# A spiking recurrence and its product with the table: the first piece of the last step taken from v itself, and v's two tiles exchanged

## The chip, the core and the metric

The kernel runs on one core of a Trainium2 chip. The metric is the time of one execution on the device in microseconds (us). Inputs and outputs lie in the chip's main memory (HBM). TensorE is the matmul engine, VectorE (DVE in the profile) and ScalarE (ACT) work element by element, GpSimd (POOL) issues the gathers, SyncE (SP) issues most transfers, and 16 DMA engines move the data. The matmul's results lie in PSUM, a memory of eight banks of 2 KB in each of 128 partitions; everything else lies in SBUF.

## The reference

`seq` (1024 x 50 indices), `lengths` (1024) and a table of 100001 x 128 numbers come in, with `gamma` and `beta` (128 each). Row 0 of the table counts as zero.

```python
e = emb[seq]                                   # 1024 x 50 x 128
uF = cumsum(e, axis=1) / minimum(t_idx, lengths)
y = (uF - mean) * rsqrt(var + 1e-5) * gamma + beta   # mean and var over the 1024 rows
def step(v, x):                                # 50 steps
    v = v + (x - v) / 2.0
    spike = (v - 1.0 >= 0)
    v = v - spike * 1.0
    return (v, spike)
scores = mean(spikes over the steps) @ emb.T   # 1024 x 100001
```

The output has 409.6 MB. It is written once; the table has 51 MB.

## The kernel before

**Recurrence (lines 172 to 443).** Everything is kept transposed: 128 features in the partitions, the 1024 rows of the batch along the free dimension. In each of the 50 steps `gather` (L204) issues eight indirect DMAs on GpSimd, two steps ahead. TensorE transposes the eight pieces of 128 rows onto a running sum in the PSUM tiles `pre0` and `pre1` (L327), so that the prefix sum is accumulated there; `correct` (L279) subtracts what row 0 of the table put in. VectorE scales each half to `uF` (L338) and takes its statistics (L339, L345). ScalarE and VectorE make 1/sqrt of the variance in a few instructions on 128x1 (L349, L362 to L375), and `a`, which holds it times -2 times a quarter of gamma; the minus sign is met by `uF` being replaced by mean minus uF (L356). Then come the new v = 0.5 x + 0.5 v: `x` (L379, ScalarE) writes 0.5 x into the tile of the new v, `step` (L382, VectorE) adds -0.5 times `negv`, which is minus the v of the step before after its reset.

The reset is made in two instructions. `over` (L293, ScalarE) writes d = v - 1 as bf16; `rest` (L297, VectorE) makes negv = (d >= 0) - v. `spiked` (L300, VectorE) counts (v >= 1) into `count`.

v lies in PSUM, in two tiles of 1024 that take turns, "v0" in even steps and "v1" in odd ones (L385). "v1" was used once before by `zps` (read by ScalarE, L226), "v0" by `rps` (read by VectorE, L245). In steps 42 and 44 the tile "v1" that the step before has left also serves to transpose the first two parts of the table (L397 to L409), and behind the loop it serves as `po1`.

**The last step (t = 49)** is cut in pieces A (128 rows), B (512) and C (384), so that the product with piece A can start early. `rest` of piece A (L320, run in L297) and `near` = -0.5 negv + 0.5 beta (L322) come at its beginning, ahead of uF on VectorE's queue. Then `centred` = (uF - mean) times -0.25 gamma (L352), q (L366, L367), which is -2 / sqrt(var + eps) up to a second-order correction, `vA` = centred q + near (L369) and `countA` (L370, run in L300). q times `centred` is thus half of x without beta. `keep_busy` (L307) puts transposes into an unused tile `warm` between the last transposes of the loop and behind them: the latter, 16 of them, read `near` (L414).

Behind the loop come the first four products, of `countA` with two parts of the table (L424), in `po0` and `po1`, each half with its own eviction (ScalarE L430, the last one VectorE L428) and store. Among them piece B is made in `pre1` (L433 to L436, ending with `countB`), and at the end piece C in a PSUM tile `vC` of the tag "v0" (L440 to L443, ending with `countC`): ScalarE writes it, VectorE adds and counts.

**Product (lines 448 to 533).** The 98 parts of the table (1024 rows of it each) are taken in blocks of 2, 3 or 6. Each part is transposed and split in two numbers of fewer bits (`prepare`, L148), `hi` and `lo` (or `pairs`). For each of the eight groups of 128 batch rows, `product` (L157, matmul in L160) fills a PSUM tile `po` of 1024 with four matmuls, VectorE (L511) and ScalarE (L513) evict in turn into `o` in SBUF, and SyncE stores (L169). The first block starts with group 1, as group 0 was done before: `po_1_0` and `po_1_1` (group 1, parts 0 and 1), then `po_2_0`, `po_2_1` and so on. Groups 1 to 4 multiply by pieces of `countB`, groups 5 to 7 by pieces of `countC`.

**Places in PSUM.** The pools of the recurrence fill all eight banks: `pre0` and `pre1` have banks 0 and 1, `po0` (and `warm`) 2 and 3, "v1" 4 and 5, "v0" 6 and 7. The pool of the product opens when they close, with four tiles of two banks over the same eight. It waits tile by tile: an instruction that writes a new tile waits for the last readers of what lay in its banks. Its first tiles have these places:

| tile | first bank | what lay there | last read by |
|---|---|---|---|
| po_1_0 | 0 | pre0, pre1 | countB (L300) |
| po_1_1 | 6 | vC | countC (L300) |
| po_2_0 | 4 | po1 | L430, L428 |
| po_2_1 | 2 | po0 | L430 |

The schedule is written by hand: each engine runs its instructions in the order of the code. Waits are put in from the tiles that instructions read and write; for PSUM there is a wait also between two engines that only read the same banks. So d of step 48 (L393, run in L293) waits for the count that L392 put ahead of it.

Of the kernel before, what the change touches and what calls it, by code (L numbers as in the profile page):

```python
# [12 lines left out]
F32 = mybir.dt.float32  # L13
# [5 lines left out]
ALU = mybir.AluOpType  # L19

P = 128
BN_EPS = 1e-5
V_TH = 1.0
HALF = 1024
KQ = HALF // P
BANK = 512
# [13 lines left out]
def rec_kernel(  # L40
# [9 lines left out]
    nc = tc.nc  # L50
    B, T = seq.shape
# [17 lines left out]
    countA = const.tile([P, P], F32R, tag="countA", name="countA")  # L69
# [60 lines left out]
    def turned(q, pt):  # L130
        r = rows.pop(q)
        if q == 0:
            nc.vector.memset(r[0:1, :D], 0.0)
        pw = deep(q)
        for k0 in range(0, HALF, P):
            nc.tensor.transpose(pt[:, k0 : k0 + pw], r[:pw, k0 : k0 + D], ident[:pw, :pw])  # L136

    def views(q, pt, hi, lo):
        pw = deep(q)
        return (  # L140
            pt.rearrange("d (k p) -> d p k", k=KQ)[:, :pw, :],
            hi[:, : pw * KQ].rearrange("d (p k) -> d p k", k=KQ),
            lo[:, : pw * KQ].rearrange("d (p k) -> d p k", k=KQ),
        )
# [3 lines left out]
    def prepare(q, pt):  # L148
        turned(q, pt)
        split[q] = hi, lo = free.pop(0)  # L150
        vp, vh, vl = views(q, pt, hi, lo)
        nc.scalar.copy(vh, vp)  # L152
        nc.vector.tensor_tensor(vl, vp, vh.bitcast(F32), ALU.subtract)  # L153
# [18 lines left out]
    with ExitStack() as ph:  # L172
        once = ph.enter_context(tc.tile_pool(name="once", bufs=1))
# [5 lines left out]
        vp = ph.enter_context(tc.tile_pool(name="v", bufs=1, space=bass.MemoryType.PSUM))  # L179
# [5 lines left out]
        r0 = once.tile([P, D], F32, tag="r0", name="r0")  # L185
        nc.sync.dma_start(out=r0, in_=table[0:1, :].to_broadcast([P, D]))
        gb = once.tile([P, 2], F32, tag="gb", name="gb")
# [39 lines left out]
        r0hi = once.tile([P, D], F32R, tag="r0hi", name="r0hi")  # L227
# [18 lines left out]

        hgb = once.tile([P, 3], F32, tag="hgb", name="hgb")
        nc.vector.tensor_scalar_mul(hgb[:, 0:1], gb[:, 0:1], 0.25)
        nc.vector.tensor_scalar_mul(hgb[:, 2:3], gb[:, 0:1], -0.25)
        nc.vector.tensor_scalar_mul(hgb[:, 1:2], gb[:, 1:2], 0.5)  # L250
        eps = once.tile([P, 1], F32, tag="eps", name="eps")
        nc.vector.memset(eps, BN_EPS)
        less = once.tile([P, 1], F32, tag="less", name="less")
        nc.vector.memset(less, -V_TH)
        count = once.tile([P, B], BF16, tag="count", name="count")
        nc.vector.memset(count, 0.0)

        negv = once.tile([P, B], F32, tag="negv", name="negv")
# [31 lines left out]
        def over(t, v):  # L290

            d = lp.tile([P, B], BF16, tag="d", name=f"d_{t}")
            nc.scalar.activation(d, v, AF.Identity, bias=less)  # L293
            return d

        def rest(d, v, cs):
            nc.vector.scalar_tensor_tensor(negv[:, cs], d[:, cs], 0.0, v[:, cs], ALU.is_ge, ALU.subtract)  # L297

        def spiked(out, cs, v):
            nc.vector.scalar_tensor_tensor(out, v, V_TH, count[:, cs], ALU.is_ge, ALU.add)  # L300
# [3 lines left out]
        pieceA, pieceB, pieceC = slice(0, P), slice(P, P + BANK), slice(P + BANK, B)  # L304
# [6 lines left out]
        v = None  # L311
# [4 lines left out]
        for t in range(T):  # L316
            last = t == T - 1
            e = es.pop(t)
            if last:
                rest(d, v, pieceA)  # L320
                near = once.tile([P, P], F32, tag="r0", name="near")
                nc.vector.tensor_scalar(near, negv[:, :P], -0.5, hgb[:, 1:2], ALU.mult, ALU.add)  # L322
            uF = up.tile([P, B], F32, tag="uF", name=f"uF_{t}")
            bs = sp.tile([P, B // BANK, 6], F32, tag="bs", name=f"bs_{t}")
            for h, cs in enumerate(halves):
                for k in range(0, BANK, P):
                    nc.tensor.matmul(  # L327
                        pre[h][:, k : k + P],
                        lhsT=e[:, h * BANK + k : h * BANK + k + P],
                        rhs=ident,  # L330
                        start=False,
                        stop=last,
                        is_transpose=True,
                        skip_group_check=True,
                    )
                    if last and h and k + P < BANK:
                        keep_busy(ident, KQ // 2)
                nc.vector.scalar_tensor_tensor(uF[:, cs], rlen[:, cs], 1.0 / (t + 1), pre[h], ALU.max, ALU.mult)  # L338
                nc.vector.bn_stats(bs[:, h, :], uF[:, cs])  # L339
            if t + 2 < T:  # L340
                gather(t + 2)
            if not last:
                correct(t + 1, l)
            mv = sp.tile([P, 2], F32, tag="mv", name=f"mv_{t}")
            nc.vector.bn_aggr(mv, bs.rearrange("p h s -> p (h s)"))  # L345


            r = sp.tile([P, 1], F32, tag="r", name=f"r_{t}")
            nc.scalar.activation(r, mv[:, 1:2], AF.Sqrt, bias=eps)  # L349
            if last:  # L350
                centred = once.tile([P, P], F32, tag="r0hi", name="centred")
                nc.vector.tensor_scalar(centred, uF[:, :P], mv[:, 0:1], hgb[:, 2:3], ALU.subtract, ALU.mult)  # L352
                w = sp.tile([P, 1], F32, tag="w", name="w")
                nc.vector.tensor_scalar_add(w, mv[:, 1:2], BN_EPS)
            else:
                nc.scalar.activation(uF, uF, AF.Identity, bias=mv[:, 0:1], scale=-1.0)  # L356


            if t and not last:
                rest(d, v, whole)  # L360

            nc.vector.reciprocal(r, r)  # L362
            q = sp.tile([P, 1], F32, tag="q", name=f"q_{t}")
            a = sp.tile([P, 1], F32, tag="a", name=f"a_{t}")
            if last:
                nc.vector.tensor_scalar(q, w, r, r, ALU.mult, ALU.mult)  # L366
                nc.vector.scalar_tensor_tensor(q, q, 3.0, r, ALU.subtract, ALU.mult)  # L367
                vA = once.tile([P, P], F32, tag="r0n", name="vA")
                nc.vector.scalar_tensor_tensor(vA, centred, q, near, ALU.mult, ALU.add)  # L369
                spiked(countA, slice(0, P), vA)  # L370
                nc.vector.tensor_mul(a, q, hgb[:, 0:1])
            else:
                nc.vector.scalar_tensor_tensor(q, mv[:, 1:2], BN_EPS, r, ALU.add, ALU.mult)
                nc.vector.tensor_scalar(q, q, r, 3.0, ALU.mult, ALU.subtract)
                nc.vector.tensor_scalar(a, q, r, hgb[:, 0:1], ALU.mult, ALU.mult)  # L375


            def x(vt, cs):
                nc.scalar.activation(vt, uF[:, cs], AF.Identity, bias=hgb[:, 1:2], scale=a)  # L379

            def step(vt, cs):
                nc.vector.scalar_tensor_tensor(vt, negv[:, cs], -0.5, vt, ALU.mult, ALU.add)  # L382

            if not last:
                vt = vp.tile([P, B], F32, tag=f"v{t % 2}", name=f"v_{t}")  # L385
                x(vt, whole)
                if t:
                    spiked(count, whole, v)
                step(vt, whole)
                v = vt  # L390
                if t == T - 2:
                    spiked(count, whole, v)  # L392
                d = over(t, v)  # L393
                if t + 2 < T:
                    l = only(t + 2)

                if t in (T - 8, T - 6):  # L397
                    q = (t - T + 8) // 2
                    pair(q)
                    prepare(q, vp.tile([P, HALF], F32, tag="v1", name=f"pt_{q}"))  # L400
                    if q == TWICE - 1:
                        for k in range(TWICE):
                            rows[GROUP + ASIDE + k] = first[:, k, :]
                        nc.sync.dma_start(
                            out=first[:, :TWICE, :],
                            in_=table[(GROUP + ASIDE) * HALF : (GROUP + SHIFT) * HALF, :].rearrange(
                                "(q p k) d -> p q (k d)", p=P, k=KQ
                            ),
                        )  # L409
# [6 lines left out]
            nc.scalar.activation(uF[:, cs], uF[:, cs], AF.Identity, bias=mv[:, 0:1], scale=-1.0)  # L416

        po0 = accp.tile([P, HALF], F32, tag="po0", name="po_0_0")
        po1 = vp.tile([P, HALF], F32, tag="v1", name="po_0_1")
        o0 = gp.tile([P, HALF], F32, tag="e", name="o_0_0")  # L420
        o1 = gp.tile([P, HALF], F32, tag="e", name="o_0_1")
        firsts = [(q, po, o, h, cs) for q, po, o in ((0, po0, o0), (1, po1, o1)) for h, cs in enumerate(halves)]
# [14 lines left out]
        rest(d, v, pieceC)  # L437
        for f in firsts:
            first_store(*f)
        vC = vp.tile([P, B - BANK - P], F32, tag="v0", name="vC")  # L440
        x(vC, pieceC)
        step(vC, pieceC)
        spiked(countC, pieceC, vC)  # L443
# [19 lines left out]
    for c, W in enumerate(WIDTHS):  # L463
# [34 lines left out]
        for n in range(NB):  # L498
            if c == 0 and n == 0:
                continue  # L500
            pool, tag, most = turns[blocks % len(turns)]
# [51 lines left out]
```

## Time and profile before

| | us |
|---|---|
| runs shown: lowest, median, highest | 1637.56, 1643.39, 1649.35 |
| the profiled execution's own time | 1576.4 |
| its span, from the first to the last instruction | 1574.6 |
| busy in the span: TensorE | 1128.4 |
| VectorE | 949.3 |
| ScalarE | 673.4 |
| GpSimd | 380.9 |

How to read the lines that follow. In a timeline a line has the start and the time in us from the span's start, the engine, the line of the kernel, the operation, its output and inputs by the program's names, shapes, the count, and in brackets how long the engine stood idle before it and what released it. In the chain that ended last a line has the start, the time, and the engine and line; "issue" is time in which the engine waited for nothing that the profile shows. A helper's instruction has the helper's line: all of `rest` is L297, all of `spiked` L300. Ends of matmuls are modelled; their starts are of more use.

### The profile page before, as it was taken

What the parts mean: (1) busy time and instruction counts of PE and PEld (TensorE: products, weight loads), DVE (VectorE), ACT (ScalarE), POOL (GpSimd) and SP (SyncE); (2) the same over time, 40 slices, a digit from 0 to 9 for tenths busy, and PEclk for the clock granted to TensorE, in tenths of its full rate; (3) what the DMA queues carried; (4) which work ended last, traced back from release to release, by engine and by line L of the source; (5) the groups of instructions that cost most, each with busy time, mean ns of one, the idle gap of its engine ahead of it and who ended that gap; (6) DMA issues with size and microseconds to landing.
All of it is one profiled execution on the core that took longest, in us unless ns stands there. A gap on an engine that the chain in (4) does not pass through costs nothing.

```text
span 1574.6 us, 12255 instructions
## 1 busy us (share of the span) xinstructions
PE 1128.4 (72%) x4464; PEld 799.5 (51%) x4464; DVE 949.3 (60%) x1127; ACT 673.4 (43%) x697; POOL 380.9 (24%) x406
## 2 busy tenths in 40 slices
PE   4544444444445998899888878888878878888884
PEld 2211111111122766677766666666666666666663
DVE  5777777777777655666555555555555545555552
ACT  2333333333333545555444444444444444444442
POOL 7777777777776000000000000000000000000000
PEclk9999999999975999999999999898999999999998
DMA  9711111111121899999999999999999999999998
GB/s 347 264 52 54 52 54 52 53 53 54 52 79 47 337 414 414 423 413 402 428 427 429 427 426 421 421 409 429 421 428 424 402 428 429 414 423 417 426 405 354
DMA packets 51313, 488.12 MB, mean 310 GB/s; under 512 B 10079, under 2 KB 10336, under 8 KB 30004
## 3 DMA queue, kind: packets, MB, share of 16 engines
q1 hardware_dynamic: 30752, 430.86, 65.1%
q0 software_dynamic: 12800, 26.24, 5.7%
q10 hardware_dynamic: 7700, 30.23, 4.7%
q8 instruction: 35, 0.57, 0.1%
q14 instruction: 26, 0.21, 0.0%
HBM read 77.69 MB, written 409.60 MB: 309 GB/s over the span
## 4 chain that ended last, share of the span: by engine, by line
DMA 48%; POOL 18%; PE 15%; issue 8%; DVE 5%; ACT 4%; ACTq 0%; SPq 0%; POOLq 0%; DVEq 0%
DMA scores<-o 42%; POOL e L207 18%; PE po L160 14%; DMA e<-in_L_rec_emb_table,idx 6%; DVE o L511 3%; ACT o L513 3%; DVE pairs L153 1%; ACT pairs L152 0%; PE pt L136 0%; ACT hi L152 0%; DVE lo L153 0%; PE pre L327 0%; DMA idx<-in_r_seq 0%; DVE bs L339 0%; DVE uF L338 0%
## 5 line engine op out<-in xcount | busy, mean ns | idle before, releaser
L511 DVE TENSOR_SCALAR o<-po 128x1024 f32<-128x1024 f32 (+1 forms) x391 | 467.3, 1214 | 329.5 <-DMA scores<-o 187.4
L513 ACT ACTIVATE o<-po 128x1024 f32<-128x1024 f32 x391 | 392.0, 1025 | 506.0 <-DMA scores<-o 362.7
L207 POOL DMA_INDIRECT e<-in_L_rec_emb_table,idx x400 | 380.2, 951 | 123.9 <-issue 112.5
L327 PE MATMUL pre<-ident,e 128*128 128x128 f32 x400 | 179.9, 463 | 227.3 <-DMA e<-in_L_rec_emb_table,idx 227.0
L160 PE MATMUL po<-pairs,countB 128*128 128x512 f32 (+1 forms) x1120 | 292.8, 408 | 57.8 <-ACT o L513 57.8
L160 PE MATMUL po<-pairs,countC 128*128 128x512 f32 (+1 forms) x840 | 240.1, 433 | 59.4 <-ACT o L513 53.4
L160 PEld LDWEIGHTS po<-pairs,countB 128*128 128x128 f32 x1120 | 211.8, 194 | 119.2 <-ACT o L513 76.7
L327 PEld LDWEIGHTS pre<-ident,e 128*128 128x128 f32 x400 | 73.4, 184 | 337.1 <-DMA e<-in_L_rec_emb_table,idx 336.4
L160 PEld LDWEIGHTS po<-pairs,countC 128*128 128x128 f32 x840 | 168.1, 208 | 112.1 <-ACT o L513 65.5
L153 DVE TENSOR_TENSOR pairs<-pt,pairs 128x1024 fp32r<-128x1024 f32 x70 | 85.2, 1218 | 94.9 <-ACT pairs L152 94.8
L338 DVE SCALAR_TENSOR_TENSOR uF<-rlen,pre 128x512 f32<-128x512 f32 x100 | 68.3, 683 | 109.6 <-PE pre L327 109.6
L136 PE MATMUL pt<-ident,rows 128*128 128x128 f32 (+1 forms) x768 | 104.4, 281 | 9.9 <-issue 4.9
L349 ACT ACTIVATE r<-mv,eps 128x1 f32<-128x1 f32 x50 | 14.7, 295 | 223.4 <-DVE mv L345 223.4
L136 PEld LDWEIGHTS pt<-ident,rows 128*128 128x128 f32 (+1 forms) x768 | 94.1, 147 | 27.1 <-issue 10.9
L160 PE MATMUL po<-hi,countB 128*128 128x512 f32 x208 | 85.6, 411 | 15.1 <-ACT o L513 13.5
L281 PE MATMUL pre<-zT,ls 128*128 128x512 f32 x100 | 77.5, 777 | 23.2 <-DVE uF L338 19.3
L152 ACT CAST pairs<-pt 128x1024 fp32r<-128x1024 f32 x70 | 70.1, 1014 | 41.2 <-PE pt L136 41.2
L160 PE MATMUL po<-lo,countB 128*128 128x512 f32 x208 | 83.4, 401 | 0.0
L293 ACT ACTIVATE d<-v,less 128x1024 bf16<-128x1024 f32 x49 | 54.6, 1114 | 64.8 <-DVE v L382 62.3
L160 PE MATMUL po<-hi,countC 128*128 128x512 f32 x156 | 66.7, 427 | 14.1 <-ACT o L513 12.6
L379 ACT ACTIVATE v<-uF,hgb,a 128x1024 f32<-128x1024 f32 x49 | 59.2, 1208 | 30.6 <-DVE a L375 30.5
L339 DVE BATCH_NORM_STATS2 bs<-uF 128x6 f32<-128x512 f32 x100 | 69.4, 694 | 3.5
(87 smaller groups left out, 851.8 us busy)
## 6 DMA issues: line engine op xcount, KB each, us to landing
scores<-o SPq DMA_DIRECT2D x96, 3072.0 KB, 19.8
scores<-o SPq DMA_DIRECT2D x32, 1536.0 KB, 8.9
scores<-o SPq DMA_DIRECT2D x30, 1024.0 KB, 7.9
rows<-in_L_rec_emb_table ACTq DMA_DIRECT2D x19, 1536.0 KB, 29.3
scores<-o SPq DMA_DIRECT2D x8, 2896.5 KB, 17.2
rows<-in_L_rec_emb_table SPq DMA_DIRECT2D x5, 3072.0 KB, 34.9
e<-in_L_rec_emb_table,idx POOLq DMA_INDIRECT x400, 2.5
rows<-in_L_rec_emb_table SPq DMA_DIRECT2D x2, 1024.0 KB
```

The costliest lines, as they stand in the source:

```text
L136: nc.tensor.transpose(pt[:, k0 : k0 + pw], r[:pw, k0 : k0 + D], ident[:pw, :pw])
L152: nc.scalar.copy(vh, vp)
L153: nc.vector.tensor_tensor(vl, vp, vh.bitcast(F32), ALU.subtract)
L160: nc.tensor.matmul(po[:, :kw], lhsT=counts[n], rhs=part[:, k0 : k0 + kw], start=j == 0, stop=j == 1,)
L207: nc.gpsimd.indirect_dma_start(out=es[t][:, n * P : (n + 1) * P], out_offset=None, in_=table, in_offset=bass.IndirectOffsetOnAxis(ap=idx[: ...
L281: nc.tensor.matmul(pre[h], lhsT=l, rhs=zT[:, h * BANK : (h + 1) * BANK], start=t == 0, stop=False, skip_group_check=True,)
L327: nc.tensor.matmul(pre[h][:, k : k + P], lhsT=e[:, h * BANK + k : h * BANK + k + P], rhs=ident, start=False, stop=last, is_transpose=True, ...
L338: nc.vector.scalar_tensor_tensor(uF[:, cs], rlen[:, cs], 1.0 / (t + 1), pre[h], ALU.max, ALU.mult)
L339: nc.vector.bn_stats(bs[:, h, :], uF[:, cs])
L379: nc.scalar.activation(vt, uF[:, cs], AF.Identity, bias=hgb[:, 1:2], scale=a)
L511: nc.vector.tensor_scalar_mul(o[:, h0 : h0 + hw], po[:, :hw], 1.0 / T)
L513: nc.scalar.mul(o[:, h0 : h0 + hw], po[:, :hw], 1.0 / T)
```

## The change

The last step's first piece is no longer made from `d` and `negv`. At the end of step 48, behind the last count and ahead of d, VectorE makes `moved` = v + beta from v in PSUM, and `near` = (v >= 1) - moved, which is minus the reset v minus beta. With 0.5 gamma in place of -0.25 gamma in `centred`, the sum `vA` is -2 times the new v, and `countA` compares it with -2 by is_le. The exchange of v's tiles makes steps with even numbers use "v1", odd ones "v0"; `pt_0`, `pt_1` and `po1` go to "v0", `vC` to "v1". So `vC` lies in banks 4 and 5 and `po1` in 6 and 7.

```diff
-        nc.vector.tensor_scalar_mul(hgb[:, 2:3], gb[:, 0:1], -0.25)
+        nc.vector.tensor_scalar_mul(hgb[:, 2:3], gb[:, 0:1], 0.5)
...
+        beta2 = gb[:, 1:2]
...
-            if last:
-                rest(d, v, pieceA)
-                near = once.tile([P, P], F32, tag="r0", name="near")
-                nc.vector.tensor_scalar(near, negv[:, :P], -0.5, hgb[:, 1:2], ALU.mult, ALU.add)
...
-                spiked(countA, slice(0, P), vA)
+                nc.vector.scalar_tensor_tensor(countA, vA, -2.0 * V_TH, count[:, pieceA], ALU.is_le, ALU.add)
...
-                vt = vp.tile([P, B], F32, tag=f"v{t % 2}", name=f"v_{t}")
+                vt = vp.tile([P, B], F32, tag=f"v{(t + 1) % 2}", name=f"v_{t}")
...
                     spiked(count, whole, v)
+                    moved = once.tile([P, P], F32, tag="r0hi", name="moved")
+                    nc.vector.tensor_scalar_add(moved, v[:, pieceA], beta2)
+                    near = once.tile([P, P], F32, tag="r0", name="near")
+                    nc.vector.scalar_tensor_tensor(near, v[:, pieceA], V_TH, moved, ALU.is_ge, ALU.subtract)
                 d = over(t, v)
...
-                    prepare(q, vp.tile([P, HALF], F32, tag="v1", name=f"pt_{q}"))
+                    prepare(q, vp.tile([P, HALF], F32, tag="v0", name=f"pt_{q}"))
...
-        po1 = vp.tile([P, HALF], F32, tag="v1", name="po_0_1")
+        po1 = vp.tile([P, HALF], F32, tag="v0", name="po_0_1")
...
-        vC = vp.tile([P, B - BANK - P], F32, tag="v0", name="vC")
+        vC = vp.tile([P, B - BANK - P], F32, tag="v1", name="vC")
```

## The prediction

> **What bounds the kernel now.** First the stretches of the recurrence and of the stores, by busy time. Columns: us, then busy us and instructions of PE, PEld, DVE, ACT, POOL, then granted TensorE clock, DMA share, GB/s.
> ```profile
> 0.00:511.00 511.00, 243.65 (x560) 106.83 (x560) 364.57 (x630) 186.19 (x205) 380.95 (x406) 0.94 0.29 93
> 511.00:1575.00 1064.00, 884.77 (x3904) 692.65 (x3904) 584.72 (x498) 487.22 (x493) 0.00 (x0) 0.94 0.98 414
> ```
> The first 511 us belong to POOL, which issues the gathers; the other 1064 us to the stores, with the DMA engines at 0.98. Nothing that the change touches is the bound of either. It touches the seam, about ten us between them in which no transfer runs, so I read next the VectorE timeline of the last step, and then the chain that ended last across the seam.
> ```profile
> 503.72 1.23 DVE L300 SCALAR_TENSOR_TENSOR count<-v,count 128x1024 bf16<-128x1024 f32 x1
> 506.12 0.29 DVE L297 SCALAR_TENSOR_TENSOR negv<-d,v 128x128 f32<-128x128 bf16 x1 [1.18 <-ACT d L293]
> 506.45 0.29 DVE L322 TENSOR_SCALAR near<-negv,hgb 128x128 f32<-128x128 f32 x1
> 506.65 0.68 DVE L338 SCALAR_TENSOR_TENSOR uF<-rlen,pre 128x512 f32<-128x512 f32 x1
> 507.36 0.69 DVE L339 BATCH_NORM_STATS2 bs<-uF 128x6 f32<-128x512 f32 x1
> 507.97 0.67 DVE L338 SCALAR_TENSOR_TENSOR uF<-rlen,pre 128x512 f32<-128x512 f32 x1
> ```
> VectorE stands idle 1.18 us for d (ScalarE, L293). d itself starts at 504.98, only when the count of L300 has ended: both read v, and the waits put 2.6 us of ScalarE's idle time down to that count. Then come two small instructions, and only then uF's first half, whose transposes were done at about 502.5.
> ```profile
> 515.64 0.57 DVE countC L300
> 516.21 0.14 issue
> 516.34 4.81 PE po L160 x20
> ...
> 522.47 7.06 DMA scores<-o
> ```
> The chain goes through the third piece: TensorE's second product tile of the new loop, po_1_1, starts only when countC is done, though it multiplies by countB. The reason is its place: po_1_1 lies in banks 6 and 7, where vC lies. The stores on the chain follow twenty matmuls later.
> ```profile
> 516.34 0.47 PE L160 MATMUL po<-hi,countB 128*128 128x512 f32 x1 [1.31 <-DVE countC L300]
> ```
> 1.31 us of idle TensorE is the price of that sharing. Whether an earlier product can be used is in the DMA share of the next microseconds (same columns as the first table).
> ```profile
> 518.00:519.00 1.00, 1.00 (x6) 0.81 (x5) 0.77 (x1) 0.49 (x1) 0.00 (x0) 1.00 0.23 90
> 519.00:520.00 1.00, 1.00 (x6) 0.84 (x5) 0.64 (x1) 0.54 (x1) 0.00 (x0) 1.00 0.39 160
> 521.00:522.00 1.00, 1.00 (x6) 0.84 (x5) 0.82 (x1) 0.30 (x1) 0.00 (x0) 1.00 0.59 246
> 522.00:523.00 1.00, 1.00 (x6) 0.83 (x5) 0.41 (x2) 0.92 (x1) 0.00 (x0) 1.00 0.95 385
> ```
> The engines wait for data up to 522 (0.77 + 0.61 + 0.41 us idle in these three rows) and are full from there. So earlier stores are worth their time, up to about 1.8 us.
>
> **The change, part by part.**
>
> 1. *near from v, ahead of d.* Gone: L297 on piece A (289 ns), L322 (286 ns), and the wait for d. New, behind the last count, which ends at 504.95: moved (tensor_scalar, 128x128, v from PSUM) and near (scalar_tensor_tensor, 128x128). No row shows moved in just this form. Nearest are L322, 286 ns from SBUF, and L297, 289 ns with one operand in PSUM; bounds 0.23 us (the tensor_scalar of L230, 227 ns) and 0.35 us (the scalar_tensor_tensor of L369, 352 ns). I take 0.29 for each, with 0.03 us between. So moved ends at 505.27, near at 505.59; uF's first half (0.68) at 506.30, its bn_stats (0.69) at 507.02. uF's second half now waits for something else: the last transpose, which starts at 507.01 when the last gather has landed. In the step before, uF followed the start of that transpose (497.04) after 0.51 us (497.55), so it starts at 507.53 instead of 507.97. **Gain 0.44 us**, and 0.5 us of slack ahead of it, so that both bounds of the two new instructions give the same. Had nothing stood behind it, the gain would have been 1.1 us; the gather is late next.
>
> [...]
>
> 2. *d goes behind the two.* As d waited for the count that reads the same banks, it will now wait for near: 505.6 to 506.7 instead of 504.98 to 506.09. Behind it on ScalarE is the square root (509.65, for mv), and d's first reader is now L434 (511.34): 0. Its cover is 2.5 us wide; with none it would cost 0.6 us.
>
> 3. *The statistics and countA.* From uF's second half to countA and the four products of piece A every instruction stays in kind and size: is_le in place of is_ge, 0.5 in place of -0.25 in hgb. 0 each; all moves 0.44 us earlier. The 16 transposes on near (to 509.89) are issued behind the last transpose and end before countA in both: 0.
>
> 4. *Parity of v's tiles.* In the loop each v still alternates with the one before; v_0 takes the tile that zT's copy on ScalarE reads, and ScalarE itself writes v_0 later: 0. pt_0 and pt_1 (steps 42 and 44) take the other tile, still that of the v before, behind the same count (3.3 us of TensorE's waiting, both ways): 0. po1 likewise. No DMA and no gather is moved or passed; SP's stores keep their order.
>
> 5. *vC in banks 4 and 5.* The new pool hands out banks 0, 6, 4, 2 in this order to po_1_0, po_1_1, po_2_0, po_2_1. If it still does, po_1_1 lies in po1's old place and waits for the last eviction of po1 (L428, 514.31 to 515.00), and po_2_0 waits for countC. In the times of before: po_1_1 starts at about 515.1 instead of 516.34, and po_2_0 takes over the start at 516.34, with four matmuls (0.91 us at the 0.227 us between starts) behind it instead of ahead. So the wait isn't gone: it moves one tile back and shrinks from 1.31 to about 0.3 us. VectorE evicts po_1_1 right behind countC (516.2 instead of 517.55), and from po_2_0 on all is 0.91 us earlier. **Gain 0.91 us**; bounds 0 (places as before) and 1.24 us (po_1_1's own gain).
>
> Sum: 0.44 + 0.91 = 1.35 us, within the 1.8 us that the DMA engines can take up. Against the profiled execution's own 1576.4 us that is 1575.05. The median of the runs, 1643.39, is 67 us (4%) above that execution; no row shows where, so I carry the 1.35 us over unchanged: 1642.0. About 1% (16.4 us) is what a measurement of this kernel can tell from no change, so this is within it.
>
> **The rivals.**
>
> *A. The places turn with the tiles.* If the pool gives po_1_1 the banks of vC again, only part 1 is left: 1643.39 - 0.44 = 1642.95. For it: how the pool chooses isn't in the trace. Against: from a fresh pool it chooses 0, 6, 4, 2, and 6 was the last to come free, so it doesn't choose by that.
>
> *B. Hidden anyway.* The next blocks return it. For it: TensorE's clock is down at 533 to 539 and the DMA engines starve meanwhile.
> ```profile
> 532.00:533.00 1.00, 0.24 (x2) 0.13 (x1) 1.00 (x2) 0.48 (x1) 0.00 (x0) 0.80 0.95 393
> 534.00:535.00 1.00, 0.94 (x3) 0.22 (x1) 1.00 (x1) 0.40 (x1) 0.00 (x0) 0.50 0.38 156
> 537.00:538.00 1.00, 1.00 (x4) 0.80 (x3) 1.00 (x1) 0.00 (x0) 0.00 (x0) 0.50 0.36 148
> 538.00:539.00 1.00, 1.00 (x4) 0.81 (x3) 0.04 (x1) 0.43 (x1) 0.00 (x0) 0.50 0.26 106
> ```
> Over the eight microseconds from 532 the shares sum to 5.84, so such a stretch costs 2.2 us of transfer. If it falls worse after the shift, the 1.35 us are gone: 1643.4. Against: the stores ahead of it shift by the same 1.35 us.
>
> *C. Slower: more half-clock stretches.* One mechanism, TensorE's clock in the store stage. Each further stretch with the products late costs 2.2 us; from eight on (8 x 2.2 = 17.6, less 1.35: 16.3) it is at 1%, and one in each of the 20 blocks behind the first would give 1643.4 - 1.35 + 44 = 1686. For it: many groups of 60 products already take 0.28 us each in the chain (1031.54, 16.88 us). Against: idle TensorE in a block is set by its stores, which don't change; 1.35 us of shift has no reason to hit them all the same way. The mirror of it, eight stretches fewer, would give 1643.4 - 1.35 - 17.6 = 1624.4.
>
> [...]
>
> **How the numbers follow.** Forecast (both parts) 0.62; A 0.13; B 0.16; C 0.05; its mirror 0.04. Forecast, A and B lie within 1%: same 0.91; slower 0.05; faster 0.04. The range takes the runs of before as they scatter, 1637.56 to 1649.35, less 1.35 us and one stretch (2.2 us) at the low end: 1634.0; plus one stretch at the high end: 1651.6, rounded to 1652. Left out are C and its mirror, and some tails of the runs.
>
> **What would show it.** Part 1: no L297 of 128x128, VectorE without the 1.18 us idle, uF's second half released by the transpose, about 0.5 us behind its start; if instead it starts behind bn_stats, the two new instructions cost more than 0.6 us each. Part 2: d released by near, nobody waiting for d. Part 5: po_1_1 released by L428, po_2_0 by countC with about 0.3 us of idle TensorE; if po_1_1 still waits 1.3 us for countC, A is right. The chain should then show sixteen products behind countC instead of twenty. Wrong would be all of this if the recurrence's end (the last transpose, 507.01) moved, or if the store stage changed by more than some us.

## The result, and the profile after

Over 14 runs of each, taken in turn, the changed kernel has a median of 1638.68 us (1637.18 to 1646.72) and the kernel before 1640.7 us (1637.56 to 1649.35). The ratio is 0.9985, with a 95% interval of 0.9971 to 0.9999: 2.5 us less by the ratio, with an interval of about 0.2 to 4.8 us. That is well within 1%, and on the side that was forecast (1.35 us). The median itself lies 3.3 us below the forecast 1642.0, mostly because the median of the kernel before is 1640.7 over these 14 runs and was 1643.39 over the three that the prediction had.

The profiled execution of before that the prediction was worked from took 1576.4 us, and those runs took about 1640; in two later groups of runs the kernel before took about 1575 us, in a third again 1638, so times and traces are compared within a group of runs only. The lines that answer to those of before are therefore shown from the changed kernel's profile in a group of runs near 1575 (e4 below, span 1571.4 us); the changed kernel's profile from the group of runs of the 14 runs follows.

The two stretches of e4, by busy time (columns as in the prediction):
```profile
0.00:510.00 510.00, 243.59 (x560) 106.83 (x560) 364.35 (x630) 186.01 (x205) 380.72 (x406) 0.94 0.29 93
510.00:1571.00 1061.00, 883.05 (x3904) 692.01 (x3904) 585.15 (x498) 487.03 (x493) 0.00 (x0) 0.94 0.98 415
```
The recurrence is what it was, with POOL at 380.7 us of 510, and the stores still hold the DMA engines at 0.98. Only the seam has moved. VectorE's timeline of the last step in e4:
```profile
504.49 0.34 DVE L391 TENSOR_SCALAR moved<-v,gb 128x128 f32<-128x128 f32 x1
504.86 0.29 DVE L393 SCALAR_TENSOR_TENSOR near<-v,moved 128x128 f32<-128x128 f32 x1
505.07 0.68 DVE L335 SCALAR_TENSOR_TENSOR uF<-rlen,pre 128x512 f32<-128x512 f32 x1
...
507.13 0.69 DVE L335 SCALAR_TENSOR_TENSOR uF<-rlen,pre 128x512 f32<-128x512 f32 x1 [0.66 <-PE pre L324]
```
VectorE's 1.18 us of idling for d is gone. A shorter wait has come in its place, 0.66 us further down: uF's second half waits for the last transpose, which started at 506.62. And d, on ScalarE in the same profile, stands behind near:
```profile
505.19 1.11 ACT L294 ACTIVATE d<-v,less 128x1024 bf16<-128x1024 f32 x1 [3.14 <-DVE near L393]
```
ScalarE idles longer ahead of d than before (3.14 us, where it was 2.6), but no instruction waits for d in turn. Next TensorE's timeline of e4, the first matmuls of po_1_0, po_1_1 and po_2_0:
```profile
513.01 0.50 PE L160 MATMUL po<-hi,countB 128*128 128x512 f32 x1 [0.24 <-DVE countB L301]
...
514.24 0.50 PE L160 MATMUL po<-hi,countB 128*128 128x512 f32 x1
...
515.43 0.50 PE L160 MATMUL po<-hi,countB 128*128 128x512 f32 x1
```
po_1_1 now starts 1.23 us behind po_1_0 (2.51 before), in the banks where po1 lay, whose last eviction (L429) ended at 514.19. po_2_0 starts 1.19 us behind po_1_1, where four matmuls at 0.23 us would be 0.92 us; countC ended at 515.38. The waits of TensorE's weight loads (PEld) at the seam name both releasers (us in total, times, longest):
```profile
PEld po L160 <- DVE o L429: 0.5, 1, 0.5
PEld po L160 <- DVE countC L301: 0.4, 1, 0.4
```
So two small waits, each about 0.3 us by the matmuls' starts, are left of the one of 1.31 us. The chain that ended last in e4:
```profile
512.26 0.70 DVE countB L301
...
513.01 1.20 PE po L160 x4
...
514.24 5.13 PE po L160 x20
...
520.69 6.37 DMA scores<-o
```
vC and countC are off the chain; it runs from countB straight through the products. And the DMA engines in e4:
```profile
519.00:520.00 1.00, 1.00 (x6) 0.84 (x5) 0.60 (x1) 0.52 (x1) 0.00 (x0) 1.00 0.39 139
520.00:521.00 1.00, 1.00 (x6) 0.82 (x5) 0.62 (x1) 0.69 (x1) 0.00 (x0) 1.00 1.02 426
```
They are full from 520 on, where in the profile of before that was 522.

The profile of the changed kernel in the group of runs near 1640 has a span of 1636.8 us, and its last step reads otherwise. VectorE's timeline:
```profile
569.17 1.22 DVE L301 SCALAR_TENSOR_TENSOR count<-v,count 128x1024 bf16<-128x1024 f32 x1
...
571.61 0.69 DVE L336 BATCH_NORM_STATS2 bs<-uF 128x6 f32<-128x512 f32 x1
572.22 0.67 DVE L335 SCALAR_TENSOR_TENSOR uF<-rlen,pre 128x512 f32<-128x512 f32 x1
```
Here uF's second half stands right behind bn_stats, with no wait: the last transpose had started at 568.14, before the count. In that execution VectorE, not the last gather, bounds the last step. That gave a second theory.

### The profile page after: what moved, and what is told of

It reads as the page before. It is cut to its first block, busy times and chain, and to the rows that moved or that the text cites. A ratio compares the mean times of both kernels' runs of the same rounds, so it can differ in the third digit from the quotient of the medians.

```text
span 1636.8 us, 12254 instructions
## 1 busy us (share of the span) xinstructions
PE 1085.8 (66%) x4464; PEld 806.9 (49%) x4464; DVE 948.7 (58%) x1127; ACT 673.0 (41%) x697; POOL 381.1 (23%) x406
## 4 chain that ended last, share of the span: by engine, by line
DMA 42%; PE 16%; DVE 14%; another core or an unknown queue 9%; POOL 7%; issue 5%; ACT 5%; ACTq 0%; SPq 0%; DVEq 0%; POOLq 0%
DMA scores<-o 40%; PE po L160 14%; POOL e L207 7%; DVE o L512 3%; ACT o L514 3%; DVE uF L335 2%; DVE bs L336 2%; DMA e<-in_L_rec_emb_table,idx 2%; DVE v L379 2%; DVE negv L298 1%; ACT v L376 1%; PE pre L324 1%; DVE count L301 1%; DVE pairs L153 1%
## 5 line engine op out<-in xcount | busy, mean ns | idle before, releaser
L282 PE MATMUL pre<-zT,ls 128*128 128x512 f32 x100 | 78.4, 786 | 271.2 <-DVE uF L335 227.2
L282 PEld LDWEIGHTS pre<-zT,ls 128*128 128x128 f32 x100 | 29.0, 291 | 309.9 <-DVE uF L335 255.7
L324 PE MATMUL pre<-ident,e 128*128 128x128 f32 x400 | 126.8, 435 | 79.5 <-DMA e<-in_L_rec_emb_table,idx 63.0
L324 PEld LDWEIGHTS pre<-ident,e 128*128 128x128 f32 x400 | 80.4, 209 | 126.8 <-DMA e<-in_L_rec_emb_table,idx 94.7
```

The source lines that it names most:

```text
L282: nc.tensor.matmul(pre[h], lhsT=l, rhs=zT[:, h * BANK : (h + 1) * BANK], start=t == 0, stop=False, skip_group_check=True,)
L324: nc.tensor.matmul(pre[h][:, k : k + P], lhsT=e[:, h * BANK + k : h * BANK + k + P], rhs=ident, start=False, stop=last, is_transpose=True, ...
```

## The experiments

**Theory 1** is the prediction's: with near moved, the last gather is late next, so that part 1 is worth 0.44 us, and the places of part 5 are worth 0.91 us. **Theory 2**: in the groups of runs near 1640 the gathers come early in the last step, so there part 1 is worth the whole wait, 1.2 us, and the sum is 2.1 us. A third question is whether a microsecond at the seam is one at the end.

### Each part alone (e1 to e4, one group of runs)

e1 is the kernel before as it is; e4 the changed one as it is. e2 is e4 with v's tiles as before:
```diff
-vt = vp.tile([P, B], F32, tag=f"v{(t + 1) % 2}", ...)   # pt_q, po1: "v0"; vC: "v1"
+vt = vp.tile([P, B], F32, tag=f"v{t % 2}", ...)         # pt_q, po1: "v1"; vC: "v0"
```
e3 is e1 with the opposite edit.

> The kernel before, unchanged, profiled again. Theory 1 (the prediction's picture: the gathers bound the last step): a span near 1575 us, VectorE idle about 1.2 us for d, the last transpose (L327) starting at about the end of that wait, and the first half of uF behind near. Theory 2 (in the executions that are timed, near 1640 us, gathers come in bursts and VectorE itself bounds the last step): a span near 1637 us, the last transpose of step 49 started before the count of step 48 has ended, and from that count's end to countA's end 6.4 us as before, all of it VectorE's own chain. Ratio of its times to the kernel before: 1.000 within 0.0015, which is the scatter of the comparison itself.

> Only near taken from v (parts 1 to 3), the tiles of v as before. From the end of step 48's count to the end of countA (6.4 us in the profile of before): theory 1 has it shortened by 0.44 us only where the last gather lands late, theory 2 has 5.2 us whenever the last transpose came early, a gain of 1.2 us. po_1_1 still waits 1.3 us for countC. Time: theory 1 ratio 0.9997, theory 2 0.9993.

> Only the tiles of v exchanged (parts 4 and 5), near from negv as before. Both theories: po_1_1 starts about 1.2 us earlier against po_1_0 and po_2_0 waits about 0.2 to 0.3 us for countC; from po_1_0's first matmul to po_2_1's first 3.5 us instead of 4.4; from the count's end to countA's end 6.4 us as before. Time: ratio 0.9994 (0.9 us).

> The changed kernel again, beside the three others on one chip. Theory 1: ratio 0.9992 (1.35 us). Theory 2: 0.9987 (1.2 + 0.9 = 2.1 us). From the count's end to countA's end 5.2 us, from po_1_0's first matmul to po_2_1's first 3.5 us.

The kernel before took 1575.23 us in this group (33 runs). Ratios with intervals: e1 1.0002 (0.9993 to 1.0011), e2 0.9997 (0.9988 to 1.0006), e3 0.9993 (0.9984 to 1.0002), e4 0.9992 (0.9983 to 1.0001), which is 1.28 us by the medians. The times can't tell these apart; the traces can. The last transpose and countA in e1, and then in e4:
```profile
506.83 0.33 PE L327 MATMUL pre<-ident,e 128*128 128x128 f32 x1
510.80 0.29 DVE L300 SCALAR_TENSOR_TENSOR countA<-vA,count 128x128 fp32r<-128x128 f32 x1
...
506.62 0.48 PE L324 MATMUL pre<-ident,e 128*128 128x128 f32 x1
510.24 0.29 DVE L367 SCALAR_TENSOR_TENSOR countA<-vA,count 128x128 fp32r<-128x128 f32 x1
```
The start of the last transpose lies between 506.27 and 507.01 in the nine profiles near 1575 us, and differs by up to 0.33 us within this group, so absolute times scatter by about as much as part 1 is worth, and only distances are compared. Worked out from the timelines, in us:

| | last transpose's start to countA's end | count's end to countA's end | po_1_0's to po_2_1's first matmul |
|---|---|---|---|
| before, profile of the prediction | 4.34 | 6.40 | 4.43 |
| e1, before | 4.26 | 6.41 | 4.43 |
| e2, near only | 3.91 | 6.01 | 4.42 |
| e3, swap only | 4.32 | 6.42 | 3.45 |
| e4, both | 3.91 | 5.96 | 3.46 |
| after, group of runs near 1640 | 7.47 | 5.22 | 3.47 |

From countA's end to po_1_0's first matmul it is 2.48 us in all six. So the two parts add up without touching each other: near from v gives 0.35 to 0.43 us (e2, e4 against e1 and the first row), the exchange 0.97 us. In e2 the wait that the exchange removes stands as it was:
```profile
515.40 0.47 PE L160 MATMUL po<-hi,countB 128*128 128x512 f32 x1 [1.32 <-DVE countC L301]
```
From the last transpose to po_2_1 it is 4.26 + 2.48 + 4.43 = 11.17 us in e1 and 3.91 + 2.48 + 3.46 = 9.85 in e4: 1.32 us. The expectation of theory 2 for e1, a span near 1637, didn't hold here, nor for e4 its 5.2 us: this group of runs is of the prediction's kind, and theory 1 is right in it.

### The last gather taken out (e5, e6) and the third piece in two other places (e7, e8)

```diff
-e = es.pop(t)
+e = e if last else es.pop(t)
...
-if t + 2 < T:
+if t + 2 < T - 1:
     gather(t + 2)
```
e5 has this in the kernel before, e6 in the changed one: step 49's rows are not gathered, step 48's are used in their place. e7 and e8 are the changed kernel with vC elsewhere:
```diff
-vC = vp.tile([P, B - BANK - P], F32, tag="v1", name="vC")
+vC = accp.tile([P, B - BANK - P], F32, tag="po0", name="vC")    # e7; e8: tag="pre0"
```

> The kernel before with the gather of step 49 left out (the last step adds the rows of step 48 once more, so part of the input is not read). Theory: before the change the last step hangs on the wait for d, not on the gather: the last transpose comes early, and from the end of step 48's count to the end of countA it is 6.4 us as ever; ratio 1.000 (0 within 0.3 us). Rival (the last gather bounds the last step in before too): countA up to 0.5 us earlier against the count's end, 5.9 us.

> The changed kernel with the gather of step 49 left out in the same way. Theory (with near taken from v the gather is late next): from the count's end to countA's end 5.2 us instead of 6.0, the first half of uF right behind near and the second right behind bn_stats; 0.8 us earlier than the changed kernel; time ratio 1 - (0.4 + 0.8 + 1.0)/1575 = 0.9986. Rival (VectorE's own chain is as long as the gather's): 6.0 us as in the changed kernel, 0.9991.

> The changed kernel with the third piece in banks 2 and 3 (where po0 was, evicted before), the place of po_2_1, the fourth tile of the new pool. Theory (the price follows the place): no tile waits for countC; from po_1_0's first matmul po_1_1 starts at 1.23 us, po_2_0 at about 2.2 (2.42 in the changed kernel), po_2_1 at about 3.2 (3.46); ratio 0.9990, 0.2 to 0.3 us below the changed kernel, under what the times can tell. Rival (the wait moves on to the fourth tile): po_2_1 still at 3.46.

> The changed kernel with the third piece in bank 0, the place of po_1_0, the first tile of the new pool. Theory: po_1_0 itself waits for countC, about 2.5 us later than in the changed kernel, and everything behind it too: from countA's end to po_1_0's first matmul 4.9 us instead of 2.5, and po_2_1's first matmul 1.8 us later than in the changed kernel, 0.9 us later than before. Time ratio: 1 + (1.8 + 1.0 - 0.4 - 1.0 - 0.9 + 0.4)/1575, about 1.0003 to 1.0010. Rival (transfers hide it): 0.9992 as the changed kernel.

This group of runs was one near 1640 (before 1638.15 us, 29 runs). e5, VectorE's timeline:
```profile
563.74 0.29 DVE L297 SCALAR_TENSOR_TENSOR negv<-d,v 128x128 f32<-128x128 bf16 x1 [1.18 <-ACT d L293]
...
564.26 0.68 DVE L338 SCALAR_TENSOR_TENSOR uF<-rlen,pre 128x512 f32<-128x512 f32 x1
```
e6, the same:
```profile
563.23 0.29 DVE L393 SCALAR_TENSOR_TENSOR near<-v,moved 128x128 f32<-128x128 f32 x1
563.43 0.68 DVE L335 SCALAR_TENSOR_TENSOR uF<-rlen,pre 128x512 f32<-128x512 f32 x1
```
From the count's end (562.55 and 562.93) to uF's first half it is 1.71 us in e5 and 0.50 in e6, to countA's end 6.42 and 5.20 us: with the gather out of the way part 1 is worth 1.2 us, as both theories need, and the kernel before has its 6.4 us with the last gather (e1) and without it (e5). So before the change the gather didn't bound the last step, and after the change it does wherever it lands late; the changed kernel of the first group of runs near 1640 (5.22 us) and e7 in this one (5.21) are as short as e6 with the gather in place, because there it lands early. e8 isn't: it has 7.82 us, as VectorE stood idle 2.5 us ahead of uF's first half for something that the trace doesn't name (the last section comes back to it), and behind such a wait near's place can make no difference. Ratios: e5 0.9985 (0.9973 to 0.9998), e6 0.9962 (0.9947 to 0.9977). Between them 0.0023 or 3.8 us, where 1.2 and 0.97 us were expected, 2.2 us; the intervals leave room for it. That e5 itself is 2.5 us below before was not expected (0.3 us): in that group of runs taking eight gathers out saves something ahead of the last step, and no run says more of it.

e7 measured 0.9989 (0.998 to 0.9999), e8 1.0013 (1.0 to 1.0026), 3.5 us apart by the medians. The wait follows the place. e8, TensorE's wait for countC (us in total, times, longest):
```profile
PE po L160 <- DVE countC L301: 2.5, 1, 2.5
```
In e7 no tile waits for countC. So the four places that vC can take among the new pool's first four tiles cost 2.5 us (first tile, e8, where the first products' matmuls start up to 0.43 us apart), 1.3 (second, before), about 0.3 (third, changed) and 0 (fourth, e7). The distances of e7 and e8 can't be read against the expectation: in these profiles, and in e6, the first products ran slower: matmuls that start 0.23 us apart in before start 0.43 us apart here, in e7 at a granted clock of 0.50. TensorE's timeline in e7:
```profile
567.29 1.97 PE L310 MATMUL warm<-ident,near 128*128 128x128 f32 x16 [1.03 <-DVE near L393]
572.00 0.51 PE L160 MATMUL po<-hi,countA 128*128 128x512 f32 x1 [2.75 <-DVE a L368]
...
572.73 0.63 PE L160 MATMUL po<-hi,countA 128*128 128x512 f32 x1
573.16 0.63 PE L160 MATMUL po<-lo,countA 128*128 128x512 f32 x1
```
and the microseconds of e7 with the granted clock (PE busy, clock, DMA share, GB/s):
```profile
571.00:572.00 1.00, 0.00 (x0) 1.00 0.00 0
572.00:573.00 1.00, 1.00 (x3) 0.66 0.00 0
573.00:574.00 1.00, 1.00 (x3) 0.50 0.00 0
```
Here the last transposes came early, and the sixteen that read near ran at full clock (1.00 in each microsecond from 567 to 570), so they were over 2.75 us before the first product; in the products the granted clock is 0.66 and then 0.50, and matmuls start 0.43 us apart instead of 0.23. po_1_0 then starts 3.44 us behind countA instead of 2.48. In e6 TensorE was slower from the sixteen on: behind 2.42 us of idle TensorE they took 3.09 us (1.97 in e7), and the first products' matmuls start 0.43 us apart:
```profile
563.57 3.09 PE L310 MATMUL warm<-ident,near 128*128 128x128 f32 x16 [2.42 <-DVE near L393]
568.28 0.77 PE L160 MATMUL po<-hi,countA 128*128 128x512 f32 x1 [1.62 <-DVE a L368]
```
In the changed kernel's profile near 1640 the sixteen stand behind 2.62 us of idle TensorE and took 3.48 us, with a granted clock of 0.50 from 572 to 574, but it was 1.00 again at 575, before the first product.

### What a microsecond at the seam is worth, and a further version (e9 to e12, one group of runs)

e9 is the changed kernel with this ahead of the last uF:
```diff
+if last:
+    for _ in range(8):
+        nc.vector.tensor_tensor(negv, rlen, rlen, ALU.add)
```
e10 is the changed kernel with more transposes, e11 has these and vC as in e7, e12 is the changed kernel as it is.
```diff
 keep_busy(near, 2 * KQ)
+keep_busy(centred, 6)
```

> The changed kernel with eight additions of 128x1024 on VectorE ahead of the last step's uF (into negv, which is written anew before it is read), about 1.2 us each by the row of 128x1024 tensor_tensor, 9.7 us in all. Theory (a microsecond at the seam is a microsecond of the whole, as the stores are bound from there): from the count's end to countA's end 9.2 to 9.7 us longer than in the changed kernel, and the time longer by as much: ratio to before 1 + (9.5 - 1.35)/T, 1.0052 for T near 1575, 1.0047 near 1638. Rival (the store stage hides part of what comes late or early): half of that or less, below 1.0025.

> The changed kernel with six more transposes into warm behind the sixteen, which read centred and so come late, shortly ahead of the first products. Theory: TensorE's idle time ahead of the first product (1.2 to 2.8 us in the profiles) falls to about 1 us or less, the first products keep the full clock where it had dropped, and from countA's end to po_1_0's first matmul it is 2.5 us in every execution; time 0 to 1 us below the changed kernel, ratio 0.9986 to 0.9992. Rival (they run past countA and hold the first products up): from countA's end to po_1_0 over 2.7 us.

> The six transposes and the third piece in po0's banks together. No tile waits for countC, po_2_1's first matmul 3.2 us behind po_1_0's (3.46 in the changed kernel) at full clock. Time 0.2 to 1.3 us below the changed kernel: ratio 0.9984 to 0.9991. Rival: no better than the changed kernel, 0.9992.

> The changed kernel beside the three others on one chip: ratio 0.9992 where the executions last about 1575 us (the gather bounds the last step), 0.9986 where they last about 1638 us (VectorE bounds it).

Before took 1575.04 us here (27 runs), e12 1573.11: 0.999 (0.9981 to 0.9999). e9 took 1584.12 us, 1.0059 (1.0045 to 1.0073), 11.0 us above e12. Its count and countA:
```profile
503.14 1.23 DVE L301 SCALAR_TENSOR_TENSOR count<-v,count 128x1024 bf16<-128x1024 f32 x1
...
519.22 0.29 DVE L370 SCALAR_TENSOR_TENSOR countA<-vA,count 128x128 fp32r<-128x128 f32 x1
```
countA ends 15.14 us behind the count, 9.16 later than in e12, and the first products, whose matmuls start 0.43 us apart, put po_1_0 another 1.2 us back: 10.4 us at the seam for 11.0 at the end. The rival (half or less) is out: what is late at the seam passes to the end in full. For what is early only the small steps speak, with wide intervals: 1.32 us in the traces of e1 and e4, and 1.28 us by the medians of before and e4, between 0.2 us longer and 2.7 us shorter (e12: 0.2 to 3.0 us shorter).

e10 took 1571.97 us, 0.9982 (0.9973 to 0.9991), e11 1572.53, 0.9987 (0.9978 to 0.9996). Both are below before; against e12 the intervals overlap. TensorE's idle time ahead of the first product fell in e10 to 0.58 us (1.83 us in e12):
```profile
510.33 0.47 PE L160 MATMUL po<-hi,countA 128*128 128x512 f32 x1 [0.58 <-DVE a L368]
```
But in this group the first products kept their pace without them too: from countA's end to po_1_0 it is 2.48 us in e10 and 2.47 in e12. So the seam doesn't explain e10's 1.1 us, and whether they help near 1640, where the first products ran slower in e6 to e8, wasn't tried. In e11 po_2_1 starts 3.16 us behind po_1_0 (3.45 in e12): the rest of the wait is gone in the trace, 0.29 us, and not to be seen in the time.

## Why the prediction was right

The measured median lies in the range of 1634 to 1652 us, but so do rival A, rival B and no change at all: the scatter of the runs makes that range 18 us wide. What speaks for the mechanism is the traces. The intervals of the ratios are about 0.15% to either side, finer than the 1% that the prediction allowed a measurement.

- *Part 1.* The wait for d went, and uF's second half is released by the last transpose 0.51 us behind its start, as forecast. 0.35 to 0.43 us against 0.44. moved took 0.34 us, not 0.29: at the upper bound, and inside the slack. That v lies in PSUM doesn't explain it alone: in the changed kernel's profile near 1640 moved took 0.341 us, against 0.286 for L322 of the kernel before, from SBUF (their forms differ), but near took 0.291 with v in PSUM, and countA (L367), of the same kind and size with all its operands in SBUF, 0.292.
- *Part 1 in the other groups of runs.* The sentence that without the gather the gain would be 1.1 us describes three of the four profiles of the changed kernel and its variants near 1640: 1.2 us (after, e6, e7; not e8). The forecast took the gather to be late in the runs shown too, and of the three of these profiles that have the last gather (after, e7, e8) it is in none what the last step waits for. That is the term that was mis-sized for them, 0.44 us for up to 1.2, and with it the sum: up to 1.2 + 0.97 = 2.2 us, against 2.5 measured (0.2 to 4.8, so the runs alone don't choose between 1.35 and 2.2). That the time still came out inside the range is owed to the range's width: the forecast's picture of the last step is not that of the runs that were timed. The note that the runs lay 67 us above the profile was the place to stop: another order of events could be behind it, and it was.
- *Parts 2 to 4.* d 0.6 us later, at no cost; no other group changed.
- *Part 5.* The places were handed out in the same order, so rival A fell. 0.97 us against 0.91, with 0.27 us left of the wait at po_2_0, about the 0.3 forecast. One of the signs didn't come: the chain doesn't run through countC with sixteen matmuls, it runs through countB with twenty-four.
- *Rivals B and C.* e9's lateness reached the end in full, so the next blocks don't return it. The first products ran slower, all or some of their matmuls 0.43 us apart instead of 0.23, in e6 to e9 and in no other profile. The idle time just ahead of them doesn't decide it: it was 1.62 us in e6 and 1.83 in e12, where they kept their pace; in e7 it was 2.75. What decides it no run shows, so that idle TensorE sets the half-clock stretches, on which the argument against C leans, was the author's estimate. As to C: in the store stage, in steps of 1 us, the granted clock falls below 0.75 in 27 separate stretches in before and e1, 28 and 27 in e4 and e12, and 33 in e10. No run shows eight more or fewer, and e10, with six more than e12, was 1.1 us faster by the medians, where 2.2 us for each would be 13 us more. So the price that the prediction took for a further stretch, in C and in the ends of its range, is not borne out.

## What to carry to other kernels

Where a loop and a stream meet, look for waits that come from places and not from data: vC cost 2.5, 1.3, 0.3 or 0 us by which bank it lay in. When a wait is taken away, price it by what is late next, and ask whether that is late in the runs that count: if the profile and the timed runs differ by several per cent, take a second profile before trusting the profile's order of events. Behind a stream that held the DMA engines at 0.98, 10.4 us more at its beginning were 11.0 us more at the end.

## What the runs showed of the hardware that was not expected

The same kernel takes 1575 us in some groups of runs and 1640 in others, and the difference lies in the recurrence: 575 us instead of 510 in the changed kernel, with the store stage the same (1062 and 1061 us). The three later groups ran on three chips, the two near 1575 on chips 7 and 15 and the one near 1640 on chip 14; whether it goes by the chip is not shown, as each of the three served one group. The waits of the changed kernel's profile near 1640 (us in total, times, longest):
```profile
DVE uF L335 <- remote: 124.4, 18, 10.0
POOL e L207 <- remote: 50.0, 10, 5.8
```
In e4 neither line exists. "remote" is what the trace can't name. Theory 2 took it for gathers that come in bursts; that falls, as GpSimd issues one about every 1.25 us all through such a wait (445.98 to 460.96). In the profile near 1640 a step reads (TensorE's last transpose of uF's first half, then VectorE's uF):
```profile
448.48 0.48 PE L324 MATMUL pre<-ident,e 128*128 128x128 f32 x1 [0.78 <-DMA e<-in_L_rec_emb_table,idx]
...
461.56 0.69 DVE L335 SCALAR_TENSOR_TENSOR uF<-rlen,pre 128x512 f32<-128x512 f32 x1 [9.67 <-remote]
```
The rows had landed and the transpose is recorded as done by 449, and VectorE, idle since 451.9, starts only at 461.56. GpSimd's unnamed waits, most of them about 5 us, come some 45 or 90 us apart in much of the recurrence, and like those of uF they stand in instructions that wait for TensorE also by name (GpSimd 13.7 us for L282, uF 16.5 us for L324). While VectorE stands, GpSimd gathers up to two steps ahead, which fits the last gather's being early there. What holds VectorE up stays open (records of matmuls are modelled, and some can be missing); it isn't the change, as the kernel before shows both times.
